# Expert layer of a decoder block: the last 96 rows of the down product in row tiles over four tiles, the gate-up product stored and read back by pairs

## The chip, the cores and the metric

One core of a Trainium2 chip runs the whole program. Its engines work side by side, each on its own queue in order: TensorE (matrix products; in the profile PE, and PEld for its weight loads), VectorE (DVE), ScalarE (ACT), GpSimd (POOL) and SyncE (SP), which here only issues transfers. TensorE reads the on-chip memory SBUF (128 partitions) and writes the accumulation banks of PSUM; transfers between SBUF and device memory (DMA) are issued by SyncE, ScalarE and GpSimd and run on 16 DMA engines. Engines wait for each other by semaphores. The metric is the device time of the program in microseconds.

## The reference, cut to what matters

The program is a decoder block on 32 sequences of 128 tokens with 512 features (4096 tokens): differential self attention, cross attention with rotary positions, and a mixture of experts. Only the expert part matters here: 32 experts, each token goes to 6 of them.

```python
sel_flat = selected_experts.ravel()              # 4096 * 6 entries
sort_idx = jnp.argsort(sel_flat)
xs = jnp.repeat(x, K, axis=0)[sort_idx]          # tokens sorted by expert
g = jax.lax.ragged_dot(xs, w_gate, group_sizes)  # [*, 512] @ [512, 352]
u = jax.lax.ragged_dot(xs, w_up, group_sizes)    # [*, 512] @ [512, 352]
d = jax.lax.ragged_dot(jax.nn.silu(g) * u, w_down, group_sizes)  # [*, 352] @ [352, 512]
expert_out = jnp.sum(d[unsort_idx].reshape(T, K, H) * weights[..., None], axis=1)
shared = jax.nn.silu(x @ sw_gate) * (x @ sw_up) @ sw_down
return (expert_out + shared).reshape(B, S, H)
```

All of it is float32. The inner width of an expert is M = 352 = 128 + 128 + 96.

## The kernel before

The program runs in stages: self attention; cross attention with the router; the shared experts of the first three of eight groups of tokens; the experts (`Experts.run`, L1508 of the profiled kernel); then the shared experts of the other five groups (`Shared.group`), which add the expert sums and write the output.

The router sorts the entries into tiles of 128 tokens of one expert each. There are 208 tiles (`usual`); a block for more of them stands behind a condition (`tc.If(many > usual)`) and is not entered with these inputs. The tiles are laid out in four lanes (`SETS = 4`): tile i belongs to lane i % 4 and uses that lane's weight buffers `wg`, `wu`, `wd`; a lane goes through its experts in order, and a weight transfer moves data only where the tile's expert is a new one (`cond=new`).

What is done to one tile, with the names of the methods:

- `tokens` (L1416): GpSimd gathers the rows of 128 tokens from `h3_d` with four indirect transfers into `e_xr`, of which there are three buffers.
- `turn_in` (L1430): VectorE transposes 32x32 blocks so that features lie on partitions (`e_xT`).
- `gate_up` (L1439): TensorE makes gate and up products (2 x 4 matrix products, each two instructions in the trace, 352 columns) in a PSUM buffer of two banks; ScalarE takes Silu of the gate half (L1451), VectorE multiplies with the up half into `gu_s` (L1452), one buffer padded to 4 x 96 columns, and ScalarE's queue stores it to device memory (`e_gu_d`, L1454) in pieces of 96 columns.
- `part_out` (L1459): ScalarE's queue reads it back as `e_gr`, so that partition groups hold pieces of columns; `turn_out` (L1468): VectorE transposes it in two instructions (96 and 32 partitions) to `e_guT`, now with the inner width on partitions.
- `down` (L1478): three products accumulate over chunks of 128, 128 and 96 rows (six instructions in the trace, 512 columns); ScalarE scales the result by the routing weight into `e_y` (L1487, two buffers); GpSimd adds it to the rows of `sum_d` in device memory with an indirect transfer that accumulates (L1488). `sum_d` is one tensor for all tiles, and the framework orders two transfers that write it: a scatter waits until the one before it has landed.

`run` fixes the order of TensorE, VectorE, ScalarE and GpSimd by hand (`manual_schedule`), so each queue follows the order of the calls. Iteration i is: products of gate and up of tile i; `turn_in` of tile i + 2; `turn_out` of tile i - 1; SyncE's loads of gate and up weights for tile i + 4; `down` of tile i - 2 with its scatter; SyncE's loads of the down weights for tile i + 2; `part_out` of tile i; `tokens` of tile i + 5. GpSimd's queue therefore reads: scatter, four gathers, scatter, four gathers and so on.

PSUM has eight banks, handed out as four buffers of two (`Common.banks`). The lists `p2`, `s_pool` and the like are pools of SBUF buffers; a pool that is opened where another was closed takes over its memory, and its first writers wait for the last readers there. After the loop all engines pass the condition, and TensorE's first product of the next stage (L1215) waits there for ScalarE's last result of the experts.

Of the kernel before, what the change touches and what calls it, by code (L numbers as in the profile page):

```python
# [10 lines left out]
F32 = mybir.dt.float32  # L11
I32 = mybir.dt.int32
AF = mybir.ActivationFunctionType
ALU = mybir.AluOpType
# [4 lines left out]
P = 128  # L19
E = 512  # L20
# [1244 lines left out]
class Experts:  # L1265
# [12 lines left out]
    RUN = 96  # L1278

    def __init__(  # L1280
# [18 lines left out]
        self.wd = [cp.tile([P, len(M_CHUNKS), E], F32, name=f"wd{s}") for s in range(SETS)]  # L1299

        self.gu_s = cp.tile([P, self.Q * self.RUN], F32, name="e_gu")

# [4 lines left out]
        self.xr, self.xT, self.gu, self.gr, self.guT = {}, {}, {}, {}, {}  # L1307

    def fetch(self):

        nc = self.cm.nc
        for j in range(self.NT):
            self.got[j] = [
                self.p2.tile([P, E], F32, name=("e_y", "e_xT")[j % 2])[:, 0 : 2 * P].rearrange(
                    "p (s o) -> p s o", o=2
                )
                for i in range(len(self.table_ds))
            ]
            for t, table_d in zip(self.got[j], self.table_ds):
                nc.gpsimd.indirect_dma_start(  # L1320
                    out=t.rearrange("p s o -> p (s o)"),
                    out_offset=None,
                    in_=table_d.rearrange("(n s) o -> n (s o)", s=P),
                    in_offset=bass.IndirectOffsetOnAxis(ap=self.rows[:, j : j + 1], axis=0),
                    bounds_check=table_d.shape[0] // P - 1,
                )
        nc.gpsimd.memset(self.gu_s, 0.0)
        nc.gpsimd.iota(self.row_i, pattern=[[0, 2]], base=self.T + 1, channel_multiplier=1)
# [71 lines left out]
    def weights_out(self, i):  # L1400

        if i >= self.end:
            return
        e, new = self.expert.pop(i)
        wd, src = self.wd[i % SETS], self.w_out[ds(e, 1)]
        top = (self.Q - 1) * 32
        m = (self.Q - 1) * self.RUN
        self.cm.nc.sync.dma_start(
            out=wd[0:top], in_=src[:, 0:m, :].rearrange("o (p c) m -> p (o c) m", p=top), cond=new
        )  # L1410
        self.last = self.cm.nc.sync.dma_start(
            out=wd[top:P, 0:2, :], in_=src[:, m:M, :].rearrange("o (p c) m -> p (o c) m", c=2),
            cond=new,
        )
# [24 lines left out]
    def gate_up(self, i):  # L1439
# [5 lines left out]
        for half, w in enumerate((self.wg[s], self.wu[s])):  # L1445
# [4 lines left out]
        act = self.p2.tile([P, M], F32, name="e_act", bufs=1)  # L1450
        nc.scalar.activation(act, pgu[:, 0, 0:M], AF.Silu)  # L1451
        nc.vector.tensor_tensor(self.gu_s[:, 0:M], act, pgu[:, 1, 0:M], ALU.mult)  # L1452
        self.gu[i] = self.dram.tile([self.Q, P, self.RUN], F32, name="e_gu_d")
        nc.scalar.dma_start(  # L1454
            out=self.gu[i].rearrange("q s m -> s q m"),
            in_=self.gu_s.rearrange("s (q m) -> s q m", q=self.Q),
        )

    def part_out(self, i):  # L1459


        gr = self.gr[i] = self.p2.tile([P, self.Q, self.RUN], F32, name="e_gr")
        self.cm.nc.scalar.dma_start(
            out=gr.rearrange("p t m -> p (t m)"),
            in_=self.gu.pop(i).rearrange("q (i t) m -> (q i) (t m)", t=self.Q),
        )

    def turn_out(self, i):  # L1468
        g = self.gr.pop(i)
        t = self.guT[i] = self.p2.tile([P, len(M_CHUNKS), P], F32, name="e_guT")  # L1470
        top = (self.Q - 1) * 32
        for rows, n in ((slice(0, top), 3), (slice(top, P), 2)):
            self.cm.nc.vector.transpose(  # L1473
                t[rows, 0:n, :].rearrange("p c (t i) -> p c t i", t=self.Q),
                g[rows, :, 0 : 32 * n].rearrange("p t (j c) -> p c t j", c=n),
            )

    def down(self, i):  # L1478
        nc = self.cm.nc
        py = self.cm.banks()[:, 0, :]  # L1480
        t, s = self.guT.pop(i), i % SETS
        for c, (_, n) in enumerate(M_CHUNKS):
            nc.tensor.matmul(  # L1483
                py, t[:n, c, :], self.wd[s][:n, c, :], start=c == 0, stop=c == len(M_CHUNKS) - 1
            )
        y = self.p2.tile([P, E], F32, name="e_y")
        nc.scalar.mul(y, py, self.weight[:, i : i + 1])  # L1487
        nc.gpsimd.indirect_dma_start(  # L1488
# [8 lines left out]
    def begin(self, first, end):  # L1497

        self.first, self.end, self.last = first, end, None
        for i in range(first, first + SETS):  # L1500
            self.weights_in(i)
            self.weights_out(i)

# [4 lines left out]
    def run(self):  # L1508


        first, en = self.first, mybir.EngineType
        with self.cm.tc.manual_schedule(engines={en.PE, en.DVE, en.Activation, en.Pool}):
# [3 lines left out]
            for i in range(first, self.end + 2):  # L1516
                self.gate_up(i)
                self.turn_in(i + 2)
                if first < i <= self.end:
                    self.turn_out(i - 1)  # L1520
                self.weights_in(i + SETS)
                if i > first + 1:
                    self.down(i - 2)
                    self.weights_out(i - 2 + SETS)
                if i < self.end:
                    self.part_out(i)
                self.tokens(i + 5)


@with_exitstack  # L1530
def decoder_kernel(
# [31 lines left out]
    with tc.tile_pool(name="x_w", bufs=1, side="right") as x_w:  # L1563
# [32 lines left out]
        p2 = ctx.enter_context(tc.tile_pool(name="x_p2", bufs=2, reuse_waits="tile"))  # L1596
        cross.run(p2)
        x_ctx.close()
        s_pool = ctx.enter_context(tc.tile_pool(name="s_p", bufs=1, reuse_waits="tile"))
# [42 lines left out]
    experts.run()  # L1642
    many = nc.values_load(used[0:1, 0:1], min_val=1, max_val=n_tiles)
    with tc.If(many > usual):
        experts.begin(usual, n_tiles)
        experts.first_tokens()
        experts.run()
# [62 lines left out]
```

## Time and profile before

| | us |
|---|---|
| median of 13 runs | 3915.15 (3905.71 to 3921.94) |
| the profiled execution | 3906.63 |
| its span, first to last instruction | 3904.9 |
| before the expert loop | 0 to 2023.6 |
| expert loop, 208 tiles | 2023.6 to 3612.2 |
| shared experts of five groups | 3612.2 to 3904.9 |

Busy time in us of each engine in these three stages, the granted clock of TensorE and the mean busy share of the 16 DMA engines:

| stage | PE | PEld | DVE | ACT | POOL | clock | DMA |
|---|---|---|---|---|---|---|---|
| before the loop | 1955.0 | 1010.6 | 1488.5 | 1421.3 | 1187.6 | 0.99 | 0.18 |
| expert loop | 1539.2 | 866.5 | 536.1 | 239.2 | 1165.8 | 1.00 | 0.70 |
| after the loop | 287.4 | 131.4 | 33.6 | 18.8 | 1.6 | 1.00 | 0.18 |

How to read the profile's lines: a group's line gives the source line, the engine, the operation, the buffers written and read (out<-in), how many, then the busy time in us and the mean of one in ns, and behind the second bar the time in which the engine stood idle just before these instructions and what ended most of it. "issue" is time in which the engine waited for nothing that the profile shows. A line of the waits gives who waited for whom: us in total, how often, the longest. A line of the instructions in order of time gives the start, the duration, the engine, the line, and how many instructions are merged in it; in brackets the idle time before. Instructions that only issue a transfer, wait, or set registers are not counted as busy. A TensorE instruction's duration contains its pipeline; what one costs in a row of them is the distance of the starts.

### The profile page before, as it was taken

Reading aid. Unit: us, or ns where it says so; the run is one execution under the profiler, and the core shown is the slowest. Engines: PE = TensorE matmul, PEld = TensorE weight load, DVE = VectorE, ACT = ScalarE, POOL = GpSimd, SP = SyncE. Lnnn points to the kernel's source line nnn. Section 1 sums busy time; section 2 is a strip of 40 time slices with the busy share of each in tenths; the row PEclk is TensorE's granted clock in tenths of the full one; section 3 lists DMA queues with packets and bytes.
Section 4 is the critical chain, followed back from the end, with each engine's and each line's share of the span. In section 5 each row is a group of like instructions: output and inputs, shape, how many; then the busy total and the mean of one; then the engine's idle time right before and its main releaser. Section 6 shows DMA issues by size and latency. Waiting matters only on the chain. (4 is left out here: it accounts for less than half of the span.)

```text
span 3904.9 us, 58185 instructions
## 1 busy us (share of the span) xinstructions
PE 3781.6 (97%) x19060; PEld 2008.4 (51%) x19060; DVE 2058.1 (53%) x3202; ACT 1679.2 (43%) x4032; POOL 2354.9 (60%) x2582
## 2 busy tenths in 40 slices
PE   8999999899999999999999999999999999999999
PEld 5666666434444444444445555555555555555444
DVE  5888888877777777776133333333333333333111
ACT  6989998757677766776101111111111111111000
POOL 3545555636777777775347777777777777775000
PEclk9999999999999999999999999999999999999999
DMA  3111110121111111111157777767767676766210
GB/s 110 34 34 36 39 34 26 44 87 51 59 56 48 45 49 50 50 47 47 55 176 169 164 165 167 168 162 165 164 145 179 152 177 149 178 153 157 80 64 32
DMA packets 285987, 387.21 MB, mean 99 GB/s; under 512 B 147888, under 2 KB 179248, under 8 KB 285616
## 3 DMA queue, kind: packets, MB, share of 16 engines
q0 software_dynamic: 62912, 109.85, 16.0%
q1 hardware_dynamic: 81792, 190.98, 15.3%
q10 hardware_dynamic: 140976, 82.60, 7.6%
q8 instruction: 154, 2.52, 0.3%
q14 instruction: 153, 1.25, 0.1%
HBM read 617.52 MB, written 143.07 MB: 195 GB/s over the span
## 5 line engine op out<-in xcount | busy, mean ns | idle before, releaser
L1422 POOL DMA_INDIRECT e_xr<-h_d,e_run_of x832 | 851.6, 1024 | 281.6 <-issue 270.9
L695 DVE TENSOR_REDUCE nm<-ps 128x2 f32<-128x1024 f32 x512 | 611.1, 1216 | 113.0 <-PE ps L691 105.7
L1452 DVE TENSOR_TENSOR e_gu<-e_act,ps 128x352 f32<-128x352 f32 x208 | 108.4, 521 | 979.5 <-ACT e_act L1451 535.7
L718 ACT ACTIVATE xp<-ps 128x1024 f32<-128x1024 f32 x512 | 506.0, 1021 | 264.1 <-PE ps L691 196.2
L1483 PE MATMUL ps<-wd,e_guT 128*128 128x512 f32 (+1 forms) x1248 | 575.7, 597 | 32.9 <-ACT e_y L1487 11.8
L714 PE MATMUL ps<-xqn,xk 32*128 32x512 f32 x2048 | 528.8, 622 | 20.8 <-ACT xp L718 19.3
L1447 PE MATMUL ps<-wg,e_xT 128*128 128x352 f32 x1664 | 530.3, 461 | 12.3 <-DMA wg<-in_L_ffn_w_gate_dram 9.9
L1447 PE MATMUL ps<-wu,e_xT 128*128 128x352 f32 x1664 | 526.8, 459 | 2.9 <-DMA wu<-in_L_ffn_w_up_dram 2.4
L691 PE MATMUL ps<-xk,xq 32*128 32x512 f32 x2048 | 526.8, 631 | 0.2 <-DVE nm L695 0.2
L1451 ACT ACTIVATE e_act<-ps 128x352 f32<-128x352 f32 x208 | 96.5, 464 | 930.2 <-PE ps L1447 421.5
L1447 PEld LDWEIGHTS ps<-wg,e_xT 128*128 128x128 f32 x1664 | 315.4, 190 | 250.4 <-issue 116.3
L1488 POOL DMA_INDIRECT sum_d<-e_y,e_into x208 | 336.0, 1615 | 169.4 <-ACT e_y L1487 81.5
L1447 PEld LDWEIGHTS ps<-wu,e_xT 128*128 128x128 f32 x1664 | 315.5, 190 | 181.0 <-DMA wu<-in_L_ffn_w_up_dram 5.4
L279 ACT ACTIVATE s<-s,a_nm 128x128 f32<-128x128 f32 x1024 | 395.8, 395 | 5.3 <-DVE a_nm L265 5.3
L1483 PEld LDWEIGHTS ps<-wd,e_guT 128*128 128x128 f32 (+1 forms) x1248 | 235.6, 191 | 288.6 <-issue 232.7
L1487 ACT ACTIVATE e_y<-ps,e_weight 128x512 f32<-128x512 f32 x208 | 143.0, 687 | 430.1 <-PE ps L1483 262.0
L714 PEld LDWEIGHTS ps<-xqn,xk 32*128 32x128 f32 x2048 | 169.0, 184 | 285.2 <-ACT xp L718 124.6
L1473 DVE STREAM_TRANSPOSE e_guT<-e_gr 96x384 f32<-96x384 f32 (+1 forms) x416 | 230.8, 555 | 64.6 <-DMA e_gr<-e_gu_d 43.9
L228 POOL TENSOR_SCALAR k<-kz,a_keep,a_extra 128x256 f32<-128x256 f32 x128 | 83.1, 658 | 286.1 <-ACT kz L227 286.1
L1028 POOL DMA_INDIRECT table_d<-entry,at x192 | 202.6, 1055 | 64.3 <-issue 52.6
L729 PE MATMUL ps<-xp,v 128*32 128x512 f32 x2048 | 233.0, 595 | 7.9 <-ACT xp L718 7.6
L1434 DVE STREAM_TRANSPOSE e_xT<-e_xr 128x512 f32<-128x512 f32 x208 | 226.6, 1089 | 8.4 <-DMA e_xr<-h_d,e_run_of 8.4
(272 smaller groups left out, 5278.3 us busy)
## 6 DMA issues: line engine op xcount, KB each, us to landing
wg<-in_L_ffn_w_gate_dram SPq DMA_DIRECT2D x208, 704.0 KB
wu<-in_L_ffn_w_up_dram SPq DMA_DIRECT2D x208, 704.0 KB
wd<-in_L_ffn_w_down_dram SPq DMA_DIRECT2D x208, 576.0 KB
e_gu_d<-e_gu ACTq DMA_DIRECT2D x208, 192.0 KB
e_gr<-e_gu_d ACTq DMA_DIRECT2D x208, 192.0 KB
wd<-in_L_ffn_w_down_dram SPq DMA_DIRECT2D x208, 128.0 KB
e_xr<-h_d,e_run_of POOLq DMA_INDIRECT x832
xres<-in_x_dram SPq DMA_DIRECT2D x32, 256.0 KB
```

The lines of the kernel that those rows point to most:

```text
L279: nc.scalar.activation(s[:, j, c, side, :], s[:, j, c, side, :], AF.Exp, bias=nm[n][:, side, at : at + 1], accum_out=sm[n][:, to : to + 1],)
L691: self.nc.tensor.matmul(sc[:, i, :], q[rows, ts(c, P)], k[rows, :], start=True, stop=True)
L695: self.nc.vector.tensor_reduce(at[:, self.ROW[side], 2 * pair : 2 * pair + 2], sc, AX.X, ALU.max, negate=True)
L714: self.nc.tensor.matmul(sc[:, i, :], k[rows, ts(c, P)], q[rows, :], start=True, stop=True)
L718: self.nc.scalar.activation(e, sc, AF.Exp)
L729: self.nc.tensor.matmul(po[b, side][ts(j, 32), :], self.v2[b % 2][:, c, 2 * j + side, :], es[j // 2][:, j % 2, :], start=c == 0, stop=c == ...
L1422: self.cm.nc.gpsimd.indirect_dma_start(out=xr[:, t, :], out_offset=None, in_=self.h3_d.rearrange("t (q f) -> (t q) f", q=self.Q), in_offse ...
L1434: self.cm.nc.vector.transpose(xT.rearrange("p c (t i) -> p c t i", t=self.Q), self.xr.pop(i).rearrange("p t (j c) -> p c t j", c=EC),)
L1447: nc.tensor.matmul(pgu[:, half, 0:M], t[:, c, :], w[:, c, :], start=c == 0, stop=c == EC - 1)
L1473: self.cm.nc.vector.transpose(t[rows, 0:n, :].rearrange("p c (t i) -> p c t i", t=self.Q), g[rows, :, 0 : 32 * n].rearrange("p t (j c) -> ...
L1483: nc.tensor.matmul(py, t[:n, c, :], self.wd[s][:n, c, :], start=c == 0, stop=c == len(M_CHUNKS) - 1)
L1488: nc.gpsimd.indirect_dma_start(out=self.sum_d[:, :], out_offset=bass.IndirectOffsetOnAxis(ap=self.into[:, i : i + 1], axis=0), in_=y[:, :] ...
```

## The change

It is made in the experts' loop alone, with the buffers moved that it needs.

- The inner width is cut in 256 (`TOP`) and 96 (`LEFT`) columns. `down` now makes two full chunks of 128 rows. The last 96 rows are left to `ends_down`, once per four tiles: the 96 rows of each of the four lanes lie as 3 x 32 on the lane's own 32 partitions (`ends` for the weights, `e_endT` for the product), and twelve products of 32 rows go into the four tiles' accumulators, chunk by chunk, lane by lane.
- The accumulators of four tiles (two PSUM buffers, two tiles in each) therefore stay until the group's `ends_down`. `leave` (ScalarE's scaling into `e_y`, now four buffers) and `scatter` (GpSimd's adding transfer) are calls of their own: two tiles' results are taken out in the iteration that ends the group, two in the next one. In such an iteration the first scatter stands ahead of `tokens` of tile i + 5 and the second behind it.
- The product of gate and up is kept for two tiles in two buffers (`e_gu`, `e_left`), stored once per pair by two transfers (pieces of 64 and of 96 columns), read back by two, in the next iteration, and transposed one iteration after that by three instructions. The padding of `gu_s` and its memset are gone.
- `down` of a tile comes four iterations behind its gate and up products, where it came two behind; the down weights of a tile are loaded in the matching iteration, and those of the last 96 rows for the next four tiles after the group.
- The pools of the cross attention and of the shared experts are closed before the loop, and a new one (`e_p3`) is opened in their memory; the shared experts get a new pool after the loop.

The core of the diff:

```diff
     Q = 4
-    RUN = 96
+    RUN, LEFT = 64, 96
+    TOP = Q * RUN
...
-        self.wd = [cp.tile([P, len(M_CHUNKS), E], F32, name=f"wd{s}") for s in range(SETS)]
-
-        self.gu_s = cp.tile([P, self.Q * self.RUN], F32, name="e_gu")
+        self.wd = [cp.tile([P, self.TOP // P, E], F32, name=f"wd{s}") for s in range(SETS)]
+        self.ends = cp.tile([P, self.LEFT // 32, E], F32, name="wd_ends")
...
-        self.cm.nc.sync.dma_start(
-            out=wd[0:top], in_=src[:, 0:m, :].rearrange("o (p c) m -> p (o c) m", p=top), cond=new
-        )
         self.last = self.cm.nc.sync.dma_start(
-            out=wd[top:P, 0:2, :], in_=src[:, m:M, :].rearrange("o (p c) m -> p (o c) m", c=2),
+            out=self.ends[ts(i % SETS, 32)],
+            in_=self.w_out[ds(e, 1)][:, self.TOP : M, :].rearrange("o (p c) m -> p (o c) m", p=32),
             cond=new,
         )
...
-        act = self.p2.tile([P, M], F32, name="e_act", bufs=1)
+        act = self.p3.tile([P, M], F32, name="e_act")
         nc.scalar.activation(act, pgu[:, 0, 0:M], AF.Silu)
-        nc.vector.tensor_tensor(self.gu_s[:, 0:M], act, pgu[:, 1, 0:M], ALU.mult)
...
+        for t, m in zip(self.gu[i // 2], (slice(0, self.TOP), slice(self.TOP, M))):
+            nc.vector.tensor_tensor(t[:, n, :], act[:, m], pgu[:, 1, m], ALU.mult)
+        if n or i == self.end - 1:
+            self.store(i // 2, n + 1)
...
+        nc.scalar.dma_start(
+            out=gu_d[0:n].rearrange("n q s m -> s (n q) m"),
+            in_=gu[:, 0:n].rearrange("s n (q m) -> s (n q) m", q=self.Q),
+        )
+        nc.scalar.dma_start(out=left_d[0:n].rearrange("n s m -> s n m"), in_=left[:, 0:n])
...
+    def ends_down(self, tiles):
+
+        t, last = self.endT.pop(tiles[0] // SETS), self.LEFT // 32 - 1
+        for c in range(last + 1):
+            for i in tiles:
+                rows = ts(i % SETS, 32)
+                self.cm.nc.tensor.matmul(
+                    self.py[i // 2][:, i % 2, :], t[rows, c, :], self.ends[rows, c, :],
+                    start=False, stop=c == last,
+                )
...
+        y = self.p3.tile([P, E], F32, name="e_y", bufs=4)
+        nc.scalar.mul(y, self.py[i // 2][:, i % 2, :], self.weight[:, i : i + 1])
...
-            for i in range(first, self.end + 2):
+            done = []
+            for i in range(first, end + 5):
                 self.gate_up(i)
                 self.turn_in(i + 2)
-                if first < i <= self.end:
-                    self.turn_out(i - 1)
+                if i % 2 and i // 2 - 1 in self.gr:
+                    self.turn_out(i // 2 - 1)
                 self.weights_in(i + SETS)
-                if i > first + 1:
-                    self.down(i - 2)
-                    self.weights_out(i - 2 + SETS)
-                if i < self.end:
-                    self.part_out(i)
+                j = i - 4
+                if first <= j < end:
+                    self.down(j)
+                    self.weights_out(j + SETS)
+                    if j % SETS == SETS - 1 or j == end - 1:
+                        group = range(j // SETS * SETS, j + 1)
+                        self.ends_down(group)
+                        for n in group:
+                            self.ends_in(n + SETS)
+                        done += group
+                ready = [(n, self.leave(n)) for n in done[:2]]
+                del done[:2]
+                if i % 2 == 0 and i // 2 - 1 in self.written:
+                    self.part_out(i // 2 - 1)
+                for n, y in ready[:1]:
+                    self.scatter(n, y)
                 self.tokens(i + 5)
+                for n, y in ready[1:]:
+                    self.scatter(n, y)
+            for n in done:
+                self.scatter(n, self.leave(n))
...
-    experts.run()
+    x_out.close()
+    e_out = ExitStack()
+    p3 = e_out.enter_context(tc.tile_pool(name="e_p3", bufs=2, reuse_waits="tile"))
+    experts.run(p3)
...
+    e_out.close()
+    shared.use(ctx.enter_context(tc.tile_pool(name="s_p", bufs=1, reuse_waits="tile")), s_w)
```

## The prediction

> **What bounds the kernel now.** I read the page first, for the share of each engine and the groups of the expert stage (its loop runs from 2023.6 to 3612.2 us, 1588.6 us of a span of 3904.9). Then the waits of TensorE and GpSimd in that stage, and last the instructions one by one, in the order of time, of these two engines.
>
> ```profile
> span 3904.9 us, 58185 instructions
> ...
> PE 3781.6 (97%) x19060; PEld 2008.4 (51%) x19060; DVE 2058.1 (53%) x3202; ACT 1679.2 (43%) x4032; POOL 2354.9 (60%) x2582
> ...
> L1422 POOL DMA_INDIRECT e_xr<-h_d,e_run_of x832 | 851.6, 1024 | 281.6 <-issue 270.9
> ...
> L1488 POOL DMA_INDIRECT sum_d<-e_y,e_into x208 | 336.0, 1615 | 169.4 <-ACT e_y L1487 81.5
> ```
>
> The page makes TensorE the bound at 97%. But the two GpSimd groups are not 851.6 + 336.0 = 1188 us of work: before nearly every gather stands 0.33 us (270.9 / 820) in which the engine waited for nothing, and that comes back with every instruction. In time order:
>
> ```profile
> 2597.00 1.62 POOL L1488 DMA_INDIRECT sum_d<-e_y,e_into  x1 [1.02 <-issue]
> 2598.93 1.06 POOL L1422 DMA_INDIRECT e_xr<-h_d,e_run_of  x1 [0.30 <-issue]
> 2600.29 1.01 POOL L1422 DMA_INDIRECT e_xr<-h_d,e_run_of  x1 [0.31 <-issue]
> 2601.60 1.01 POOL L1422 DMA_INDIRECT e_xr<-h_d,e_run_of  x1 [0.30 <-issue]
> 2602.92 1.01 POOL L1422 DMA_INDIRECT e_xr<-h_d,e_run_of  x1 [0.30 <-issue]
> 2604.24 1.62 POOL L1488 DMA_INDIRECT sum_d<-e_y,e_into  x1 [0.30 <-issue]
> ```
>
> A scatter takes 1.92 us to the next start, a gather 1.32: one tile is 2604.24 - 2597.00 = 7.24 us of GpSimd's queue, without a wait in it. TensorE beside it:
>
> ```profile
> 2052.54 2.74 PE L1483 MATMUL ps<-wd,e_guT 128*128 128x512 f32 x6
> 2055.12 2.53 PE L1447 MATMUL ps<-wg,e_xT 128*128 128x352 f32 x8
> 2057.49 2.53 PE L1447 MATMUL ps<-wu,e_xT 128*128 128x352 f32 x8
> 2059.86 2.74 PE L1483 MATMUL ps<-wd,e_guT 128*128 128x512 f32 x6
> ```
>
> The undisturbed tile is 7.32 us on TensorE (gate and up 4.74, down 2.58, so 0.43 per instruction of the down product). Over the stage a tile takes 1588.6 / 208 = 7.64 us. So two queues run neck and neck, GpSimd 0.08 us ahead. GpSimd's waits, and its last three instructions, with nothing but scatters left:
>
> ```profile
> POOL sum_d L1488 <- ACT e_y L1487: 79.7, 39, 5.8
> ...
> POOL sum_d L1488 <- DMA sum_d<-e_y,e_into: 7.2, 4, 2.2
> ```
>
> ```profile
> 3602.88 1.55 POOL L1488 DMA_INDIRECT sum_d<-e_y,e_into  x1 [5.76 <-ACT e_y L1487]
> 3608.36 1.55 POOL L1488 DMA_INDIRECT sum_d<-e_y,e_into  x1 [3.93 <-issue]
> 3613.85 1.55 POOL L1488 DMA_INDIRECT sum_d<-e_y,e_into  x1 [3.94 <-issue]
> ```
>
> This is the row that decides. All scatters add into one tensor, sum_d, so each waits until the one before has landed. With no gathers between them they start 5.48 us apart, though e_y of the second was finished at 3605.24. In the loop four gathers (5.32 us) stand between two scatters and cover that: only 7.2 us are left of it.
>
> **The change part by part.**
>
> *Down product (TensorE).* Per four tiles the third chunk goes (8 instructions, 8 x 0.43 = 3.44 us) and 24 instructions of 32 rows come. If four run at a time these are 6 rounds, 2.58 us, plus the switches into and out of row tiles. The shape exists in the cross attention, four of them starting within 0.02 us, the next four 0.53 later, then 0.43 apart:
>
> ```profile
> 1501.08 0.70 PE L714 MATMUL ps<-xqn,xk 32*128 32x512 f32 x2
> 1501.09 0.70 PE L691 MATMUL ps<-xk,xq 32*128 32x512 f32 x2
> 1501.61 0.59 PE L714 MATMUL ps<-xqn,xk 32*128 32x512 f32 x2
> ```
>
> The 64-row pairs of the shared experts (L1254) hold TensorE from 3716.23 to 3717.29, 1.06 us for two rounds of 0.43, so switching costs 0.2 to 0.3. I take 2.85 us: 0.6 saved per four tiles, 31 us over 52 groups. Bounds: 0 if switching eats it; 45 if it is free. TensorE then needs 4 x 4.74 + 16 x 0.43 + 2.85 = 28.7 us for four tiles. The Trainium skill, "TensorEngine Tiling (Array Packing)", Key Properties, says that a change of tiling mode drains TensorE; it gives no price, L1254 gives one, and by neither does TensorE become the bound.
>
> *Pairs, one tile later.* Down runs four tiles behind gate and up instead of two. TensorE's waits at L1483 sum to 32.6 us (11.8, 10.7, 5.7, 3.4, 1.0 by releaser) and those at L1447, for weights, to 15.1. The first are late e_guT or wd; with some 20 us instead of 14 from product to use most would go: 0 to 33 us, I take 28. The 15.1 stay.
>
> *What hides.* ScalarE issues two stores and two readbacks per pair instead of one and one per tile: the same number, 0.37 and 0.34 us each, on an engine busy 239 of 1588.6 us. VectorE splits one product in two and does three transposes per pair for four: it is busy 536 us. SyncE issues four weight loads per tile as before, the four of the last rows together after a group. PSUM holds two pairs of results longer; each product still gets the bank of two tiles earlier. Stores are cut into 256 and 384 bytes for 384: 640 pieces per tile for 512, on a queue that takes 7.6% of the DMA engines. All 0; without its cover ScalarE's part would be about 1.4 us per tile. The new pools wait for the shared experts' last store at the start: 0 to 2 us, and I take 0.
>
> *Scatters (GpSimd).* The count is the same, the order is not. Results come out once per four tiles, two in the iteration that ends the group, two in the next. With the loop's order the queue reads, per four tiles: scatter, 4 gathers, scatter, **scatter**, 4 gathers, scatter, 8 gathers. The second and third scatter stand side by side, and nothing covers the landing. Behind the waiting third stand the gathers of the next tiles, for which VectorE's transposes (e_xT) and TensorE's next products wait. The cycle is 4 x 7.24 = 28.96 us plus the spacing of the two instead of 1.92. Bounds of the spacing: 5.48 (the idle tail) and 7.24 (the median distance of the loop's scatters, the queue's own beat, so landing under load is mostly shorter). I take 5.6, near the tail, since it is the same pair of instructions: 28.96 + 5.6 - 1.92 = 32.6 us. That is above TensorE's 28.7 and above the 30.5 of before (1588.6 / 52). So GpSimd is the bound, both gains above turn into idle TensorE, and VectorE waits for gathers.
>
> The skill's page "DMA: Bandwidth & Descriptors", Anatomy of one DMA, fits a GpSimd DMA by 2.0 us + bytes / 436 KB per us, for 256 KB an estimate of 2.6 us. By it the spacing would be about 2.9, the cycle 29.9, and the change a gain of some 30 us; the tail's 5.48 is the measured one.
>
> *Sum.* Start at 2023.6; four iterations of 4.74, three of 6.46, one of 9.31 and a leave bring the first scatter to 2072.3. Until the last gathers 49 cycles follow: 49 x 32.6 = 1597 us, to 3669.7. Then the drain. Eight scatters (tiles 196 to 203), 5.5 us apart, keep the four e_y buffers; the result of tile 207 can only leave when that of 203 has landed, 7 x 5.5 + 5.4 = 44 us later, and the next stage's first product waits for ScalarE's last result, as at 3612.20 now. With 1 us for this: 3714.7 instead of 3612.2, so +102.5 us. The 292.7 us behind it stay, since sum_d is needed there some 45 us later. The profiled execution took 3906.6, so it would be 4009; it lies 8.5 under the median of 3915.15, and on that basis I predict **4018 us**.
>
> **Rivals.**
>
> *Faster.* If the third scatter hardly waits, GpSimd's 28.96 and TensorE's 28.7 hold: 31 + 28 saved, 15 lost in the drain, 45 net: 3870. It decides when the spacing is under about 3.2 us (30.5 - 28.96 + 1.92, less 0.3 for the drain). For it: in the loop only 7.2 us of this wait show. Against it: there 5.32 us of gathers cover it, and no two scatters come closer than 5.48.
>
> *The wait is longer under load.* With 7.24 us the cycle is 34.2: 49 x 1.64 = 80 more, 10 to 15 more in the drain: about 4110. For it: DMA engines are busy 0.70 of this stage against an idle tail. Against: half of the loop's scatters come on the beat of 7.24, unhindered.
>
> *Row tiles run one after another.* 24 x 0.43 = 10.3 us, TensorE at 36.2 per cycle, 52 x 36.2 = 1882 us, +294: about 4210. Against: the rows of L714 and L691. Two at a time (31.0) would change nothing, as GpSimd stays above.
>
> *No change.* Spacing near 3.2 us; no row stands there.
>
> **How the numbers follow.** GpSimd's cycle with a spacing of 4.9 to 6.4: 0.78; the longer wait 0.06; serial row tiles 0.03; faster 0.10; within 0.2% (8 us, about what can be told from no change) 0.03. So slower 0.87, same 0.03, faster 0.10. The range takes the first case, 4018 less 38 and plus 42: 3980 to 4060, with 0.10 + 0.03 below it and 0.09 above.
>
> **What would show it.** Right: in time order on GpSimd one gap of 3.5 to 4 us per four tiles between two scatters, every other start 1.32 or 1.92 after the last; 32 to 33 us from group to group; TensorE under 90% in the stage, its waits at the gate product or behind VectorE's e_xT; 12 row-tiled pairs of instructions in 2.7 to 3.0 us; the last eight scatters 5.5 apart. Wrong: scatters side by side under 3.2 us apart, or TensorE still without gaps at 28.7 per four tiles.

## The result and the profile after

The changed kernel takes **4065.31 us** (median of 8 runs, 4058.58 to 4068.15), the kernel before 3912.99 us (37 runs on the same chip). The ratio is 1.0389, with a 95% interval of 1.0379 to 1.0399: slower by 3.9%. Predicted were 4018 us and 3980 to 4060. The direction and the mechanism are as predicted; the loss is 152 us where 103 were expected, so the time lies 5 us above the range.

The page of the changed kernel, the lines that answer to those shown of before (group lines: operation and count | busy us, mean ns of one | idle us ahead of them):

```profile
span 4059.2 us, 59622 instructions
...
PE 3819.1 (94%) x19892; PEld 2007.1 (49%) x19892; DVE 1990.6 (49%) x3306; ACT 1660.6 (41%) x4032; POOL 2347.4 (58%) x2581
...
L1428 POOL DMA_INDIRECT e_xr<-h_d,e_run_of x832 | 850.1, 1022 | 286.3 <-issue 241.9
...
L1550 POOL DMA_INDIRECT sum_d<-e_y,e_into x208 | 333.1, 1601 | 337.1 <-issue 193.7
```

GpSimd does the same work as before (850.1 and 333.1 us), and the idle time ahead of the scatters has doubled, from 169.4 to 337.1 us. 168 us more of idle GpSimd, on a kernel that lost 154.3 us of span: the loss shows at this place, and the experiments have to say whether it starts there. One group of four tiles, in the order of time on GpSimd:

```profile
2614.55 1.62 POOL L1550 DMA_INDIRECT sum_d<-e_y,e_into  x1 [0.30 <-ACT e_y L1543]
2616.48 1.06 POOL L1428 DMA_INDIRECT e_xr<-h_d,e_run_of  x1 [0.30 <-issue]
...
2621.81 1.61 POOL L1550 DMA_INDIRECT sum_d<-e_y,e_into  x1 [0.31 <-issue]
2627.22 1.56 POOL L1550 DMA_INDIRECT sum_d<-e_y,e_into  x1 [3.79 <-issue]
2629.08 1.08 POOL L1428 DMA_INDIRECT e_xr<-h_d,e_run_of  x1 [0.30 <-issue]
...
2634.45 1.62 POOL L1550 DMA_INDIRECT sum_d<-e_y,e_into  x1 [0.30 <-issue]
...
2646.93 1.62 POOL L1550 DMA_INDIRECT sum_d<-e_y,e_into  x1 [0.30 <-issue]
```

This is the order that was predicted: scatter, four gathers, two scatters side by side, four gathers, scatter, eight gathers. One gap of 3.79 us stands in it, ahead of the third scatter. This group takes 2646.93 - 2614.55 = 32.38 us. It is one of the short ones: from the first scatter (2075.16) to the last gather (3716.07) the 49 cycles take 33.49 on average.

TensorE near the end of the stage:

```profile
3733.47 1.88 PE L1523 MATMUL ps<-wd,e_guT 128*128 128x512 f32 x4
3735.28 2.86 PE L1534 MATMUL ps<-wd_ends,e_endT 32*128 32x512 f32 x24
3738.07 3.70 PE L1523 MATMUL ps<-wd,e_guT 128*128 128x512 f32 x8
3744.55 5.37 PE L1523 MATMUL ps<-wd,e_guT 128*128 128x512 f32 x8 [2.78 <-issue]
3749.84 2.86 PE L1534 MATMUL ps<-wd_ends,e_endT 32*128 32x512 f32 x24
3764.04 6.09 PE L1215 MATMUL ps<-s_hT,sg 128*128 128x512 f32 x8 [11.34 <-ACTq L1728]
```

The 24 row tiles take 2.79 us from their start to the next instruction's (3738.07 - 3735.28), so they do run four at a time; 2.85 was expected. The next stage starts at 3764.04, after 11.34 us of waiting for ScalarE's queue, where the kernel before started it at 3612.20: 151.8 of the 154.3 us are lost by then.

### The profile page after: what moved, and what is told of

The parts are those of the page before. It is cut to its first block, busy times and chain, and to the rows that moved or that the text cites. A ratio compares the mean times of both kernels' runs of the same rounds, so it can differ in the third digit from the quotient of the medians.

```text
span 4059.2 us, 59622 instructions
## 1 busy us (share of the span) xinstructions
PE 3819.1 (94%) x19892; PEld 2007.1 (49%) x19892; DVE 1990.6 (49%) x3306; ACT 1660.6 (41%) x4032; POOL 2347.4 (58%) x2581
## 5 line engine op out<-in xcount | busy, mean ns | idle before, releaser
L1428 POOL DMA_INDIRECT e_xr<-h_d,e_run_of x832 | 850.1, 1022 | 286.3 <-issue 241.9
L1465 DVE TENSOR_TENSOR e_gu<-e_act,ps 128x256 f32<-128x256 f32 x208 | 86.3, 415 | 1180.3 <-ACT e_act L1457 606.4
L1453 PE MATMUL ps<-wg,e_xT 128*128 128x352 f32 x1664 | 563.4, 484 | 67.9 <-ACT e_act L1457 37.3
L1550 POOL DMA_INDIRECT sum_d<-e_y,e_into x208 | 333.1, 1601 | 337.1 <-issue 193.7
L1523 PE MATMUL ps<-wd,e_guT 128*128 128x512 f32 x832 | 420.5, 629 | 89.9 <-ACT e_act L1457 82.3
L1453 PEld LDWEIGHTS ps<-wg,e_xT 128*128 128x128 f32 x1664 | 326.0, 200 | 343.8 <-issue 147.6
L1523 PEld LDWEIGHTS ps<-wd,e_guT 128*128 128x128 f32 x832 | 161.4, 198 | 254.9 <-issue 121.1
L1543 ACT ACTIVATE e_y<-ps,e_weight 128x512 f32<-128x512 f32 x208 | 131.4, 685 | 316.1 <-remote 107.4
L279 ACT ACTIVATION_READ_ACCUMULATOR s<-s,a_nm 128x1 f32 x1024 | 198.9, 194 | 0.0
```

The costliest lines, as they stand in the source:

```text
L279: nc.scalar.activation(s[:, j, c, side, :], s[:, j, c, side, :], AF.Exp, bias=nm[n][:, side, at : at + 1], accum_out=sm[n][:, to : to + 1],)
L1428: self.cm.nc.gpsimd.indirect_dma_start(out=xr[:, t, :], out_offset=None, in_=self.h3_d.rearrange("t (q f) -> (t q) f", q=self.Q), in_offse ...
L1453: nc.tensor.matmul(pgu[:, half, 0:M], t[:, c, :], w[:, c, :], start=c == 0, stop=c == EC - 1)
L1523: self.cm.nc.tensor.matmul(self.py[i // 2][:, lane % 2, :], t[:, c, :], self.wd[lane][:, c, :], start=c == 0, stop=False,)
L1550: self.cm.nc.gpsimd.indirect_dma_start(out=self.sum_d[:, :], out_offset=bass.IndirectOffsetOnAxis(ap=self.into[:, i : i + 1], axis=0), in_ ...
```

## The experiments

The theory: GpSimd's queue sets the pace, and the loss is the wait of the third scatter for the landing of the second in the same tensor. The rivals: row tiles, pairs, PSUM or the longer lag cost the time, and the gap only follows; or the third scatter waits for its input or its place. After the result a second question came up: why the cycle is 33.5 and not 32.6.

Times differ between chips: the kernel before takes 3913 us on the chip of the result, and 3865, 3853 and 3856 on the three chips of the experiments (e1 to e4; a, e5 and e6; e7 to e10). Each ratio is against the kernel before on the same chip.

| run | median us | before there | ratio (95%) |
|---|---|---|---|
| e1_one_per_turn | 3883.29 | 3865.11 | 1.0051 (1.0032 to 1.0069) |
| e2_two_tensors | 3891.60 | 3865.11 | 1.0073 (1.0050 to 1.0096) |
| e3_order_alone | 4034.41 | 3865.11 | 1.0434 (1.0412 to 1.0456) |
| e4_weights_kept | 4026.89 | 3865.11 | 1.0418 (1.0397 to 1.0439) |
| a_before_same_chip | 3851.38 (one run) | 3852.82 | |
| a_after_same_chip | 4043.89 | 3852.82 | 1.0498 (1.0484 to 1.0513) |
| e5_one_per_turn_8_buffers | 3845.15 | 3852.82 | 0.9982 (0.9973 to 0.9991) |
| e6_after_8_buffers | 4030.41 | 3852.82 | 1.0465 (1.0449 to 1.0481) |
| e7_fewer_scatters_row_tiles | 3820.22 | 3856.36 | 0.9903 (0.9886 to 0.9919) |
| e8_fewer_scatters_before | 3849.37 | 3856.36 | 0.9980 (0.9970 to 0.9990) |
| e9_weights_kept_again | 4021.35 | 3856.36 | 1.0425 (1.0408 to 1.0443) |
| e10_after_beside | 4056.74 | 3856.36 | 1.0517 (1.0500 to 1.0535) |

**One scatter per iteration.** Everything of the change stays, and only the scatters are spread:

```diff
-            done = []
+            done, out = [], []
...
-                for n, y in ready[:1]:
-                    self.scatter(n, y)
+                out += ready
+                if out:
+                    self.scatter(*out.pop(0))
                 self.tokens(i + 5)
-                for n, y in ready[1:]:
-                    self.scatter(n, y)
-            for n in done:
-                self.scatter(n, self.leave(n))
+            out += [(n, self.leave(n)) for n in done]
+            for n, y in out:
+                self.scatter(n, y)
```

> The changed kernel, with one edit: results still leave PSUM in the same iterations, but at most one scatter is issued per iteration, ahead of that iteration's gathers, and the rest are kept for the next iterations. No two scatters stand side by side in the loop. Theory A (the loss is the landing wait between two neighbouring scatters, 4.39 us idle before the third position of every group, 210 us in all): the queue's beat goes back to 7.24 us per tile, 28.96 per four, TensorE's 28.7 is as large, and the time is 3850 to 3890, below the kernel before. Rival B (row tiles, pairs, the longer lag or PSUM cause the loss, and the gap on GpSimd only follows from it): the time stays near 4065.

It takes 3883.29 us, within theory A's range. The cycle of a group of four tiles falls to 29.9 on average (median 29.3, the shortest 28.95), and the idle time ahead of the scatters falls from 337.1 us in the changed kernel's profile to this:

```profile
L1550 POOL DMA_INDIRECT sum_d<-e_y,e_into x208 | 335.7, 1614 | 154.3 <-issue 77.4
```

Row tiles, pairs and the longer lag are all still there, so they are not the loss. One part of the expectation missed: it is not below the kernel before, which is 48 us faster on this chip than on that of the result. Part of the rest is at the end, where this kernel also waits for ScalarE's queue:

```profile
3585.96 5.50 PE L1215 MATMUL ps<-s_hT,sg 128*128 128x512 f32 x8 [13.08 <-ACTq L1728]
3591.30 3.60 PE L1215 MATMUL ps<-s_hT,su 128*128 128x512 f32 x8
```

**Two tensors.** The order stays, and what two neighbours share goes:

```diff
-            out=self.sum_d[:, :],
+            out=(self.other_d if i % 2 else self.sum_d)[:, :],
...
-    x1_d = dram.tile([B, P, E], F32, name="x1_d")
+    other_d = dram.tile([T + P, E], F32, name="x1_d")
+    x1_d = other_d[0:T, :].rearrange("(b p) e -> b p e", p=P)
```

> The changed kernel with its order of scatters untouched, but the odd tiles' results are added into a second tensor (so the sums that the last stage reads lack the odd tiles' expert results). Two neighbouring scatters then share no tensor. Theory A (the third scatter waits for the landing of the second in the same tensor): the pair's spacing falls from 6.00 to about 1.92 us, the cycle of four tiles from 33.5 to about 29, the drain is halved, and the time is 3840 to 3890. Rival B (it waits for its own input e_y behind ScalarE, or for its place in the queue, not for the tensor): spacing and time stay, near 4065.

It takes 3891.6 us, 1.6 over theory A's upper end and 170 below the rival. The pair in time order on GpSimd, the first of the two adding into the other tensor:

```profile
2624.96 1.62 POOL L1550 DMA_INDIRECT x_d<-e_y,e_into  x1 [0.30 <-issue]
2626.88 1.56 POOL L1550 DMA_INDIRECT sum_d<-e_y,e_into  x1 [0.30 <-issue]
2628.75 1.09 POOL L1428 DMA_INDIRECT e_xr<-h_d,e_run_of  x1 [0.30 <-DVE e_guT L1511]
```

1.92 us apart, and 2.01 on average over the 47 groups in the middle, where the changed kernel has 6.00. So the place in the queue and the input are not what the third scatter waits for; the tensor is. The Trainium skill, "DMA: Bandwidth & Descriptors", Rules for kernel authors, asks for such a wait where the same bytes are touched: an accumulating DMA beside another access of them has to wait for the earlier DMA's semaphore. Here the wait is made for the whole tensor, and this run shows what it costs: 4 us per pair. Two parts of the expectation missed. The cycle is 30.1 where about 29 was expected, since with the landing out of the way the first scatter of 29 groups waits for its own input e_y instead, 59 us in all; and the drain, from the last gather to the next stage's first product, is 41.1 us for the changed kernel's 48.0, not half of it.

**The order alone.** The kernel before, with its own down product, no pairs and no longer lag, gets the changed order of scatters, together with the four e_y buffers and the moved pools that hold them:

```diff
+            out = []
...
-                    self.down(i - 2)
+                    out.append((i - 2, self.down(i - 2)))
...
+                now = out[:2] if i % 4 in (1, 2) and i > first + 2 else []
+                del out[: len(now)]
+                for n, y in now[:1]:
+                    self.scatter(n, y)
                 self.tokens(i + 5)
+                for n, y in now[1:]:
+                    self.scatter(n, y)
```

> The kernel before (three chunks of the down product, no pairs, no longer lag), with one part of the change alone: scatters are held back and issued in the changed kernel's order (scatter, 4 gathers, scatter, scatter, 4 gathers, scatter, 8 gathers), with four e_y buffers. Theory A: this order alone gives the loss, a cycle of 33 to 33.5 us for four tiles where the kernel before takes 30.5: 49 x 2.5 to 3.0 = 125 to 150 us, less or more some 20 for the start and the drain; so 4030 to 4070. Rival B (the order costs little without row tiles and pairs): 3905 to 3950.

It takes 4034.41 us, 4.3% or 169 us above the kernel before, with a cycle of 33.1. The changed kernel has cycles of 33.3 to 33.5 and loses 3.9 to 5.2% on the other chips; it was not run on this one. So the order, without row tiles, pairs or the longer lag, makes a loss of the same size and nearly the same cycle. This run also shows how to read the column of releasers. Its waits of GpSimd in the stage:

```profile
POOL sum_d L1492 <- ACT e_y L1487: 210.7, 56, 5.8
POOL sum_d L1492 <- issue: 52.5, 137, 4.0
```

and the pair in time order:

```profile
2604.74 1.61 POOL L1492 DMA_INDIRECT sum_d<-e_y,e_into  x1 [0.30 <-issue]
2610.40 1.56 POOL L1492 DMA_INDIRECT sum_d<-e_y,e_into  x1 [4.05 <-ACT e_y L1487]
```

The wait is put down to e_y, ScalarE's result, and so it is in 46 of the 48 full groups. But in each of the 48, e_y of that scatter had been finished for at least 17.9 us, 26.4 in the median (worked out from the two engines' instructions in the trace). In the changed kernel the same gap is put down to "issue" or to e_act, and there e_y was 1.8 us early at the least, 7.9 in the median. Only the run with two tensors says what the wait is for.

**Weights kept.** To find the extra 0.9 us per cycle, the largest transfers of the stage are taken out after the first four tiles:

```diff
+        never = cp.tile([P, 1], I32, name="e_never")
+        nc.gpsimd.memset(never, 0)
+        self.never = never[0:1, 0:1]
...
-                self.fresh[at], engines=[mybir.EngineType.SP], min_val=0, max_val=1
+                self.fresh[at] if i < SETS else self.never, engines=[mybir.EngineType.SP],
+                min_val=0, max_val=1,
```

> The changed kernel, but after the first four tiles no expert's weights are loaded any more (later tiles are computed with the first weights, so the results are other numbers; the instructions of every engine stay). It takes the largest transfers of the stage away. Theory A1 (the spacing of 6.00 us and the distance of 7.66 after the third scatter exceed the idle tail's 5.48 and the queue's 7.24 because the landing shares DMA engines with the weights): the cycle falls from 33.5 to about 32.6, 49 x 0.9 = 45 us less, so about 4020. Rival B1 (the excess has nothing to do with that load: the gathers, the stores, or waits for e_xr and e_y): within 10 us of 4065.

4026.89 us, with a cycle of 32.8. But the changed kernel itself had not run on this chip, and the chips differ by more than the effect, so alone this says little. It was repeated beside the changed kernel:

> The changed kernel without weight loads after the first four tiles, again, now beside the changed kernel on the same chip. From the traces so far: where no weight transfer was under way, the scatter after the pair came 7.24 us behind its third (33 of 33 in two runs), else 7.55 to 8.01 on average, and the pair's distance was 5.79 to 5.89 for 6.33 to 6.35. Theory: cycle 32.8 for 33.3 to 33.5, so 20 to 35 us less than the changed kernel. Rival: within 8 us of it.

> The changed kernel, unchanged, beside the run without weight loads: cycle 33.3 to 33.5, 4040 to 4066, 20 to 35 us above the run without weight loads if these transfers are what stretches the landings.

4021.35 and 4056.74 us: 35.4 us for the weights, where 20 to 35 were expected. The cycles are 32.77 and 33.52 on average over 47 groups, so 47 x 0.75 = 35. The idle time ahead of the scatters, first without and then with weight transfers:

```profile
L1554 POOL DMA_INDIRECT sum_d<-e_y,e_into x208 | 333.1, 1601 | 298.2 <-issue 156.8
```

```profile
L1550 POOL DMA_INDIRECT sum_d<-e_y,e_into x208 | 333.2, 1602 | 334.0 <-issue 223.4
```

The traces also show it inside one run, since a tile loads weights only where a new expert begins. In the changed kernel's trace, in the 21 groups with no weight transfer under way from 1 us ahead of the third scatter to the next, these two are 7.24 us apart (7.25 at most); in the other 26 they are 8.01 apart on average and 10.18 at most, for landings take up to 9.41 us there (the last recorded step of the landing; this trace has not kept all of them). One such place, first GpSimd and then SyncE's queue:

```profile
2551.73 1.62 POOL L1550 DMA_INDIRECT sum_d<-e_y,e_into  x1 [0.30 <-issue]
2557.96 1.56 POOL L1550 DMA_INDIRECT sum_d<-e_y,e_into  x1 [4.61 <-issue]
...
2568.08 1.62 POOL L1550 DMA_INDIRECT sum_d<-e_y,e_into  x1 [3.19 <-issue]
```

```profile
2558.19 0.35 SPq L1396 DMA_DIRECT2D wg<-in_L_ffn_w_gate_dram  x1
2558.87 0.35 SPq L1396 DMA_DIRECT2D wu<-in_L_ffn_w_up_dram  x1
```

The third scatter starts at 2557.96, new weights set out beside it, and the fourth waits 3.19 us although four gathers stand between: 10.12 us from start to start, where 7.24 are the queue's own.

**Before and after on one chip.**

> The kernel before, unchanged, for its trace beside the experiments: on the chip of the first four experiments its median was 3865 us, 48 less than on the chip of the result (3913). Theory: the difference lies in the expert stage's loop, where it waits for ScalarE's e_y behind late weights or late turns, and the stage takes about 1540 to 1550 us there instead of 1588.6. Rival: all stages are shorter in the same measure (1.2%), and the stage takes 1570.

> The changed kernel, unchanged, beside the experiments. Theory (GpSimd's cycle is set by landings and does not speed up with the rest): 4055 to 4070 here too if the cycle is 33.5 on this chip as well, so a ratio of about 1.05 where the kernel before takes 3865 and 1.039 where it takes 3913. Rival: its cycle is also shorter on this chip, about 32.7 as with the weights left out, so 4025 to 4035, and leaving out the weights was worth nothing.

The profiled kernel before has a span of 3849.6 us here, 55.3 less than on the chip of the result, and its next stage starts at 3556.92 instead of 3612.20, 55.3 earlier. So the difference between these two profiles lies in the expert stage or ahead of it; the first scatter starts at 2042.0 there and 2042.6 here, which leaves the expert stage. It takes 1532.4 us here, somewhat less than the 1540 to 1550 expected, and 1588.6 there; its cycle is 29.4 here and 30.6 there. GpSimd's waits for e_y are 81.5 us there (the group line of L1488 in the prediction), and here, from the waits of the stage:

```profile
POOL sum_d L1488 <- ACT e_y L1487: 34.0, 33, 5.8
```

The changed kernel gains less on this chip: 4043.89 us, 21 less, with a cycle of 33.3. The time fell between the two expectations; the cycle is nearer to the theory's. What the change costs is thus 3.9% on one chip and 5.0 and 5.2% on two others, mostly because the kernel before differs. Why the same kernel waits more on the one chip was not settled. The landings of its scatters do not show it (5.06 us on average there, 5.23 here), but the trace from there has kept only some of the landings' steps, so 5.06 may be too short. What the two traces do show is that ScalarE's e_act starts more than 0.5 us behind its tile's up product in 90 tiles of 208 there, and in 14 here.

**Eight buffers.** One number changes, `bufs=4` to `bufs=8` for e_y, first in the kernel with one scatter per iteration and then in the changed kernel:

> The kernel with one scatter per iteration, and eight e_y buffers for four. Its drain held the next stage's first product for 13.1 us behind ScalarE's last results, which waited for buffers of scatters not yet landed, and after that pause its first eight instructions took 5.50 us for 3.60. Theory (the drain is a matter of buffers): both go, 12 to 16 us less than with four buffers, about level with the kernel before (ratio 1.000 to 1.003). Rival (the drain is set by the landings themselves, since the last stage needs the sums): no change, 1.005.

> The changed kernel with eight e_y buffers for four, its order of scatters untouched. Theory (in the loop the landing wait alone counts, and the 47 us of the drain are a matter of buffers): the cycle of four tiles stays within 0.1 us, the next stage starts some 20 us earlier, and the time is 15 to 25 us less than the changed kernel's on this chip. Rival (e_y's buffers also hold the loop): 40 us less or more.

In the changed kernel it is worth 13.5 us (4043.89 to 4030.41), just under the 15 to 25 expected. The cycle stays (33.3 and 33.2). The next stage starts at 3728.07 for 3747.4, 19.3 us earlier, and gives some of it back. The last scatter starts at 3759.98, about when it did (3763.06), ScalarE's first result of the next stage is held until a scatter has landed, and behind that TensorE waits for what VectorE makes of it:

```profile
ACT s_act L1222 <- DMA sum_d<-e_y,e_into: 28.7, 1, 28.7
```

```profile
PE ps L1231 <- DVE s_gu L1223: 3.2, 1, 3.2
```

With one scatter per iteration the time is 3845.15 us, a ratio of 0.9982, and its interval ends at 0.9991: this version is faster than the kernel before, by 0.2%, and 199 us faster than the changed kernel on the same chip. Level to 0.3% slower was expected. From the last gather to the next stage's first product it takes 34.2 us (3515.13 to 3549.37), where four buffers took 48.5. Part of its gain against the run with four buffers may come from the other chip.

**What the row tiles are worth.** The gain of that version is small because GpSimd's queue, 28.9 us per four tiles in the median and 29.5 on average, lies above TensorE's need. To see TensorE alone, every fourth scatter is left out of this version, and of the kernel before:

```diff
     def scatter(self, i, y):
+        if i % 4 == 3:
+            return
```

> The kernel with one scatter per iteration and eight buffers, without the scatter of every fourth tile (a quarter of the experts' results is not added). GpSimd then needs 28.96 - 1.92 = 27.0 us for four tiles and lies under TensorE. Theory (row tiles save TensorE 0.6 us per four tiles, which GpSimd's queue hides): the cycle falls from 28.9 to about 28.7, TensorE's need, so 10 to 20 us less than with all scatters, some 3825 to 3835 on a chip where the kernel before takes 3853, and 25 to 35 us less than the next kernel of this call. Rival (row tiles save nothing worth naming): level with the next kernel.

> The kernel before, without the scatter of every fourth tile (a quarter of the experts' results is not added): GpSimd 27.0 us for four tiles, TensorE 4 x 7.32 = 29.28. Theory (two queues neck and neck, TensorE's three full chunks are the floor when GpSimd has room): the cycle is 29.3, as in the kernel before on a good chip, and the time within 10 us of the kernel before there (3853). Rival (GpSimd alone was the bound): 28 or less per four tiles, 50 us or more faster.

3820.22 and 3849.37 us, 29 us apart, as expected; the first is 5 us under the range given for it (25 us less than with all scatters on another chip, where 10 to 20 were expected), the second 7 us under the kernel before. TensorE is almost without gaps in both. First with row tiles, then the kernel before, from 2100 to 3500 us (columns: stretch and length, busy us and instructions of PE, PEld, DVE, ACT and POOL, granted clock, DMA share, GB/s):

```profile
2100.00:3500.00 1400.00, 1400.00 (x5051) 790.87 (x5050) 441.09 (x875) 208.91 (x391) 1021.29 (x915) 1.00 0.68 160
```

```profile
2100.00:3500.00 1400.00, 1398.55 (x4208) 798.01 (x4207) 491.06 (x766) 220.34 (x383) 1009.41 (x907) 1.00 0.68 163
```

The cycles are 28.78 and 29.25 us in the median, 28.75 and 29.29 on average; 52 x 0.54 = 28 us, so the cycle holds nearly all of the difference. And inside the first, in time order on TensorE:

```profile
2613.00 1.88 PE L1523 MATMUL ps<-wd,e_guT 128*128 128x512 f32 x4
2614.81 2.86 PE L1534 MATMUL ps<-wd_ends,e_endT 32*128 32x512 f32 x24
2617.60 2.63 PE L1453 MATMUL ps<-wg,e_xT 128*128 128x352 f32 x8
2620.07 2.53 PE L1453 MATMUL ps<-wu,e_xT 128*128 128x352 f32 x8
```

Six rounds of 0.43 would be 2.58 us. The row tiles hold TensorE for 2.79, the four instructions ahead of them for 1.81 instead of 4 x 0.43 = 1.72, and the eight behind for 2.47 (2620.07 - 2617.60) instead of the 2.37 of an undisturbed product: 0.4 us of switching in all.

## Why the prediction was right and where it was wrong

*What bounds the kernel: right.* The prediction read two queues neck and neck, GpSimd's 7.24 us per tile and TensorE's 7.32. The run without every fourth scatter leaves the kernel before at 29.25 per four tiles, 4 x 7.32 = 29.28, and the version with one scatter per iteration and eight buffers has a median cycle of 28.9 (29.5 on average), 4 x 7.24 = 28.96.

*The mechanism of the loss: right.* The order on GpSimd, the gap ahead of the third scatter, and the wait for the landing in the shared tensor are as written; the order without the other parts makes a loss of this size, and removing the shared tensor or the neighbourhood takes most of it away (ratios of 1.007 and 1.005). The signs came a little worse than given: the gap is 4.39 us on average for 3.5 to 4, the cycle 33.5 for 32 to 33, TensorE is busy 90.2% of the stage for under 90, and the eight scatters of the drain start 5.80 us apart for 5.5. The estimate from the skill's page "DMA: Bandwidth & Descriptors", Anatomy of one DMA, which put two neighbours 2.9 us apart and made the change a gain, does not hold: no pair in the changed kernel stands closer than 5.41.

*Row tiles: right in size.* 2.85 us taken, 2.79 measured, 28.7 us per four tiles against 28.78. The 31 us are 28 of the cycle when GpSimd has room; in the changed kernel TensorE waits instead.

*Stalls of the down product (28 us): not shown.* The sum lets most of the 32.6 us go; in the changed kernel TensorE waits 87 us ahead of its down product (L1523, 35 times). The column puts 79.9 of them down to e_act, but 30 of the 35 waits, 84.9 us, end 0.10 us behind a transpose into e_guT on VectorE. In the run e10_after_beside, on another chip, all 56, 153 us, do, and ahead of 55 of these transposes VectorE had waited for the gathered rows of e_xT, which is the idle TensorE that the prediction saw coming. The kernel before, on another chip, waited only 2.5 us for its down product. So these stalls were not a fixed property of the two-tile lag, and what the pairs alone gain was not measured.

*The failing step: "The cycle is 4 x 7.24 = 28.96 us plus the spacing of the two instead of 1.92", with 5.6 for the spacing.* Span to span the miss is 51.8 us (4059.2 against 4009 less the 1.7 around the span). It splits as follows:

- Start: the first scatter at 2075.16 for 2072.3, 2.9 us; the first down product waited 2.47 us and its four instructions then held TensorE for 3.33 instead of 1.72.
- Cycle: 49 cycles of 33.49 for 32.6, 43.5 us. The mean of the middle 47 groups, 33.54, has the pair 6.00 apart (taken 5.6: +0.40), the third and fourth 7.67 (taken 7.24: +0.43), and the fourth and the next first 12.63 (12.56 in the sum: +0.07; the queue's own beat is 12.48 there, and six of these starts waited for e_y, 7 us in all).
- Drain: 48.0 us from the last gather's start to the next stage for 45, 3.0 us; the drain's scatters stand 0.3 us further apart.
- Behind it: 295.2 us for 292.7, 2.5 us, since the first eight instructions after the wait ran 6.09 us for 3.70.

The pair's own spacing, 6.00, lies within the 4.9 to 6.4 that the prediction allowed, and alone would have made about 4038. What took the time out of the range is that the sum knew only one landing in the cycle, the second scatter's. "Every other start 1.32 or 1.92 after the last" did not hold: the third scatter's landing also shows, although four gathers stand behind it, and the three small terms all went the same way.

What the runs show in its place: a landing depends on what else is under way. On another chip, without weight transfers, the pair is 5.79 apart and all other starts keep the queue's beat (7.26 after the third), a cycle of 32.77; with them, on the same chip as that, 6.26 and 7.46, a cycle of 33.52. The idle tail, from which 5.6 was taken, has no such transfers. The remaining 0.2 us between 5.79 and that run's own tail (its last twelve scatters start 5.55 apart on average) are not explained by these runs; the gathers ahead of the pair may take part, which was not tried.

*The rivals and chances.* Slower was right, and the rival "the wait is longer under load" names the cause of the miss. It was set at one far value, a spacing of 7.24, and given 0.06. Load does not move one spacing from 5.6 to 7.24; it stretches the starts behind two of the four landings by 0.2 to 0.5 us on average, and up to 2.9 us in single groups (10.18 after the third for 7.24).

## What to carry to other kernels

A scatter that adds into a tensor is as long as its landing when the next one on the queue adds into the same tensor; before moving such operations, write down the queue's new order and look for neighbours. Spreading them again, one ahead of each set of gathers, with eight buffers for the end, kept the rest of this change and turned 5.0% of loss into 0.2% of gain. When a transfer's latency becomes part of the critical cycle, price it from moments when the same other transfers are in flight, not from an idle tail: here the cycle came 0.9 us longer than priced, 44 us in all, and the runs without weight loads show 0.75 us of such a difference to be these transfers.

## What was not expected of the hardware

After a pause TensorE runs at half its clock for some microseconds, and a slow GpSimd so makes TensorE slower as well. The changed kernel around the start of the next stage (columns as above):

```profile
3764.04:3767.00 2.96, 2.96 (x4) 1.41 (x5) 0.00 (x0) 0.00 (x0) 1.09 (x1) 0.50 0.48 53
3767.00:3770.10 3.10, 3.10 (x6) 1.28 (x6) 0.00 (x0) 0.00 (x0) 0.97 (x1) 0.70 0.19 34
3770.10:3773.00 2.90, 2.90 (x9) 1.23 (x8) 0.00 (x0) 0.00 (x0) 0.57 (x1) 1.00 0.66 73
```

The granted clock is 0.50 after the 11.34 us of waiting, and 1.00 again some 6 us later. From 2100 to 3500 us it is 0.96 in the changed kernel and 1.00 in the kernel before. A pause of 2.78 us was enough for it: the eight instructions at 3744.55, shown above, take 5.37 us, with a mean granted clock of 0.59 to 3747.00. The length of the pause alone does not decide: after 3.01 us ahead of 3565.24 the clock stays at 1.00. The Trainium skill, "TensorE: Matmul & The Clock Gate", What's actually happening, gives half the clock after an idle window of about 3.4 us; this trace agrees on the half, and shows it after a shorter pause too.

And the kernel before takes 3913 us on the chip of the result and 3853 to 3865 on those of the experiments, with the whole difference between its two profiles in one stage whose two queues are nearly level.
